# In-degrees of graphs 33 to 128 from a second load of the adjacency and GpSimd sums; Fourier coefficients stored in groups of four

## The chip, the cores and the metric

The kernel runs on one core of one Trainium2 chip. The metric is the device time of one execution in microseconds (us), lower being better. Times of before come from three runs; the profile is of one further execution. Engines are named as the profile names them: PE (TensorE matmuls), PEld (TensorE weight loads), DVE (VectorE), ACT (ScalarE), POOL (GpSimd), SP (SyncE, which issues most DMAs).

## The reference

128 graphs of 128 nodes with 256 features (x), and a weighted adjacency adj of 128 x 128 per graph, pass through two layers, each followed by a residual and a layer norm. All arithmetic is float32. Cut to what matters here:

```python
# layer 0, on x (128 graphs, 128 nodes, 256) and adj (128, 128, 128)
in_degrees = sum(adj, axis=-1)                       # one number per graph and node
norm  = (in_degrees + 1e-06) ** -0.5
f_hom = (adj @ ((x @ theta) * norm)) * norm
f_het = x @ W_h
gate  = sigmoid(x @ W_t + b_t)
x = layernorm(x + elu(gate * f_hom + (1 - gate) * f_het))

# layer 1
h      = relu(bn1(conv1(x)))                         # 1 x 1 convolution over the features
h      = bn2(conv2(h))                               # 17 taps along the nodes, 256 -> 256 features
x_conv = relu(h + x)
s      = x @ w_se.T + b_se
A      = exp(-pairwise_squared_distance(s)) * adj
x_nmp  = A @ relu(x @ w_msg.T + b_msg)
x = layernorm(x + GRU([x_conv, x_nmp], x))
```

## The kernel before

The kernel receives adj as `adjT` with its axes ordered (source node, graph, target node), so that a slice of it has source nodes on partitions. It works in three stages, and passes data between them through DRAM.

**Stage A** (`a_round`, lines 597 to 679, called for t = -1 to 63 at lines 681 to 683) takes the graphs in 64 pairs. Round t multiplies pair t by the three weights of layer 0 (`l0_project`), mixes it over the adjacency (`l0_mix`), and does later steps for earlier pairs: the gate, elu and norm of pair t-1, the store of x1 (the output of layer 0) of pair t-2, its reload in blocks (`load_back`, tile x1b) and its 32 x 32 block transposition on DVE (`l1_turn`, line 441, tile x1T), the first convolution of pair t-3 (`l1_front`), and, for pair t-4, the first half of the long convolution as a discrete Fourier transform over the nodes (`l1_analyse`, lines 481 to 492). That last step multiplies by a table of 136 frequencies and ACT copies the 2 x 136 coefficients of each graph from PSUM to the tile H (line 490). H stays in SBUF up to stage B. In most rounds four matmuls w_ps (`w_unit`, every second round) or a matmul wl_ps also transform conv2's weights.

The degrees of a pair are made one round ahead, in `l0_degrees` (lines 347 to 356): two TensorE transposes of its adjT tiles into a PSUM bank adj_ps (line 351), a DVE sum along the free axis (line 353), then an add and a power of -0.5 on POOL (lines 206 and 207). The result `norm` scales ACT's copy `hom` of the next round (line 380) and DVE's step behind the mix (line 402).

**Stage B** (lines 818 to 850) multiplies the coefficients by the transformed weights, one pair of frequencies k at a time, 68 in all. The stationary operand of a product is the 128 x 128 slice of H for one frequency m and one half c of the features, given by `coefs` (line 733). Each k has four such products (line 826), and all but k = 0 also two products whose stationary operand `hs` is a DVE sum of two slices of H (line 836).

**Stage C** (lines 1219 to 1258) does the way back of the transform, the message passing and the GRU. It does not touch H.

The order of the work in stage A is written out by hand for all five engines (`manual_schedule`, line 681), that of stage B for ACT and POOL, that of stage C for PE and DVE. Each engine runs its instructions in that order, and SP issues its DMAs in that order too. A float32 product issues two instructions on TensorE, each with its own weight load; a transpose issues one. H is made at t = 3 (line 670) in the space of the tiles of the setup:

```python
H = hpool.tile([P, NC, M, NB], F32, tag="H", name="H")   # 128 x (2 halves, 136 frequencies, 128 graphs)
```

Of the kernel before, what the change touches and what calls it, by code (L numbers as in the profile page):

```python
# [9 lines left out]
F32 = mybir.dt.float32  # L10
I32 = mybir.dt.int32
AF = mybir.ActivationFunctionType
ALU = mybir.AluOpType

P = 128
D = 256
NC = D // P
J = 2
# [8 lines left out]
M = L  # L27
# [3 lines left out]
DEG_EPS = 1e-6  # L31
# [3 lines left out]
def gnn_layers_kernel(ctx: ExitStack, tc: tile.TileContext, a: dict, out: bass.AP):  # L35
# [10 lines left out]
    nc = tc.nc  # L46
    x, adjT = a["x"], a["adjT"]
    NB = x.shape[0]
# [21 lines left out]
    ident = const.tile([P, P], F32, tag="ident", name="ident")  # L70
# [21 lines left out]
    K, Q = 32, P // 32  # L92
# [22 lines left out]
    for name, width, parts, pattern, base, mult in (  # L115
# [5 lines left out]
        i = setup.tile([P, width], I32, tag=f"{name}_i", name=f"{name}_i")  # L121
# [5 lines left out]
    def bank(name):  # L127
        return ps.tile([P, 512], F32, tag="ps", name=name)

    st = {}  # L130
# [225 lines left out]
        inv_sqrt(norm, norm, DEG_EPS, J)  # L356


    def l0_project(p, between, beside):
        s = st[p]  # L360
        xT, norm = s["xT"], s["norm"]
        hom = wf.tile([P, J, D], F32, tag="hom", bufs=2, name=f"hom_{p}")
        het = wk.tile([P, J, D], F32, tag="het", bufs=2, name=f"het_{p}")
        gate = wk.tile([P, J, D], F32, tag="gate", bufs=2, name=f"gate_{p}")
        pg = bank(f"gate_ps_{p}")
        for j in range(J):
            if j == 1:
                between()
            pf = bank(f"f_ps_{p}_{j}")
            for c in range(NC):  # L370
                nc.tensor.matmul(  # L371
                    pf, lhsT=xT[:, c, nodes(j)], rhs=w0[:, c, 0 : 2 * D],
                    start=(c == 0), stop=(c == NC - 1),
                )
            for c in range(NC):
                nc.tensor.matmul(  # L376
                    pg[:, j * D : (j + 1) * D], lhsT=xT[:, c, nodes(j)],
                    rhs=w0[:, c, 2 * D : 3 * D], start=(c == 0), stop=(c == NC - 1),
                )
            nc.scalar.activation(hom[:, j, :], pf[:, 0:D], AF.Copy, scale=norm[:, j : j + 1])  # L380
            nc.scalar.activation(het[:, j, :], pf[:, D : 2 * D], AF.Copy)
        beside()
        nc.vector.tensor_tensor(
            gate, pg.rearrange("p (j e) -> p j e", j=J),
            b_t.unsqueeze(1).to_broadcast([P, J, D]), ALU.add,
        )

        nc.scalar.activation(gate, gate, AF.Tanh, scale=0.5)
        s.update(hom=hom, het=het, gate=gate)
# [91 lines left out]
    def l1_analyse(p):  # L481
        h = st[p]["h"]
        for j in range(J):
            pa = bank(f"coef_ps_{p}_{j}")
            for c in range(NC):
                nc.tensor.matmul(  # L486
                    pa[:, c * M : (c + 1) * M], lhsT=h[:, j, c * P : (c + 1) * P], rhs=A,
                    start=True, stop=True,
                )
            nc.scalar.activation(  # L490
                H[:, :, :, p * J + j], pa[:, 0 : NC * M].rearrange("p (c m) -> p c m", c=NC), AF.Copy
            )


# [95 lines left out]
    H = None  # L590
    E = mybir.EngineType

    SOON = 3
    norms, ways = batch_norms(), way_back()
    tables = table(AT2, (node, lag))

    def a_round(t):
        nonlocal H
        def on(q, work):
            if 0 <= q < NP:  # L600
                work(q)

        def between():
            on(t - 1, l0_gate)
            on(t - 3, l1_turn)
            on(t - 4, l1_analyse)

        def beside():
            if 0 <= t <= SOON:
                l0_turn(t + 1)  # L610
            on(t - 1, l0_elu)
            if 0 <= t < SOON:
                l0_degrees(t + 1)

        if t > 1 and t % 2 == 1 and t + 1 < NP:
            load_blocks(t + 1, 2)
        l0_project(t, between, beside) if t >= 0 else between()
        on(t - 1, l0_norm)
        if t == 0:
            load_blocks(2, 2)  # L620
        if t == -1:
            next(tables)
        if not 0 <= t <= SOON:
            on(t + 1, l0_turn)
        on(t - 3, l1_front)
        on(t - 2, x1_store)
        if t > 0:
            load_x(t)
        if t + 2 < NP:
            if 2 <= t + 2:  # L630
                load(t + 2)
            if 3 <= t < 3 + FS:
                leftover_table(t - 3)
            if t == FS:
                v_load(0)
        else:
            on(t - 2, load_back)
            m_load(t + 2 - NP)
        if t - 1 in units:
            w_store(units[t - 1])  # L640
        if t - 1 in units_v:
            v_store(units_v[t - 1])
            if units_v[t - 1] + 1 < NV:
                v_load(units_v[t - 1] + 1)
        if t + 2 < NP:
            on(t - 2, load_back)
        on(t - 3, x1T_store)
        if not 0 <= t < SOON:
            on(t + 1, l0_degrees)
        if t == -1:  # L650
            next(tables, None)
        if t == 0:
            nc.sync.dma_start(conv1_w[:, :, 0:D], a["conv1_wT"].rearrange("(p c) e -> p c e", c=NC))
            nc.sync.dma_start(conv1_w[:, :, D:], a["w_seT"].rearrange("(p c) e -> p c e", c=NC))
            next(norms)
        if t == 1:
            next(norms)
            next(ways)
        if t == NP // 2:
            nc.scalar.dma_start(w_msg, a["w_msgT"].rearrange("(p c) e -> p c e", c=NC))  # L660
            nc.scalar.dma_start(b_msg, a["L1_gnn_b_msg"].partition_broadcast(P))
        on(t, l0_mix)
        if t == 2:
            next(norms, None)
        if t in (4, 5):
            next(ways, None)
        if t == SOON:
            sctx.close()
            hpool = hstack.enter_context(tc.tile_pool(name="hpool", bufs=1))
            H = hpool.tile([P, NC, M, NB], F32, tag="H", name="H")  # L670
        if 0 <= t < 2:
            w_load(t)
        if t - 1 in units and units[t - 1] + NW < NU:
            w_load(units[t - 1] + NW)
        if t in units_v:
            v_unit(units_v[t])
        if t in units:
            if t + 1 < NP:
                w_unit(units[t])
# [51 lines left out]
    pb = cpool("psB", 6, bctx, space=PSUM)  # L731

    def coefs(m, c):
        return H[:, c, m, :]

    left = cw.tile([P, NB, KD], F32, tag="left", name="left")
    right = cw.tile([P, NB, KD], F32, tag="right", name="right")
# [80 lines left out]
    with tc.manual_schedule(engines={E.Activation, E.Pool}):  # L818
        for k in range(M // 2):
            w = wb.tile([P, 2, NC, D], F32, tag="w", name=f"wb_{k}")  # L820
            nc.sync.dma_start(w, w_d[k].rearrange("s p c o -> p s c o"))
            py = pb.tile([P, 2, D], F32, tag="py", name=f"y_ps_{k}")
            y = yb.tile([P, 2, D], F32, tag="y", name=f"yb_{k}")
            for blk in range(2):
                for c in range(NC):
                    nc.tensor.matmul(  # L826
                        py[:, blk, :], lhsT=coefs(blk if k == 0 else 2 * k + 1 - blk, c),
                        rhs=w[:, blk, c, :], start=(c == 0), stop=(c == NC - 1),
                    )
            if k == 0:  # L830
                nc.vector.tensor_copy(y, py)
            else:
                ws = yb.tile([P, NC, D], F32, tag="ws", bufs=2, name=f"ws_{k}")
                nc.gpsimd.tensor_tensor(ws, w[:, 0], w[:, 1], ALU.add)  # L834
                hs = yb.tile([P, NC, NB], F32, tag="hs", bufs=2, name=f"hs_{k}")
                nc.vector.tensor_tensor(hs, H[:, :, 2 * k, :], H[:, :, 2 * k + 1, :], ALU.add)
                pz = pb.tile([P, 2, D], F32, tag="py", name=f"z_ps_{k}")
                for c in range(NC):
                    nc.tensor.matmul(  # L839
                        pz[:, 0, :], lhsT=hs[:, c, :], rhs=ws[:, c, :],  # L840
                        start=(c == 0), stop=(c == NC - 1),
                    )
                z = yb.tile([P, D], F32, tag="z", bufs=2, name=f"zb_{k}")
                nc.scalar.activation(z, pz[:, 0, :], AF.Copy, scale=-0.5)
                nc.vector.tensor_tensor(y, py, z.unsqueeze(1).to_broadcast([P, 2, D]), ALU.add)
            nc.sync.dma_start(y_d[:, 2 * k : 2 * k + 2, :], y)
            if k > 3 and k % 3 == 0:
                next(rest, None)
        for _ in rest:
            pass  # L850
# [369 lines left out]
    with tc.manual_schedule(engines={E.PE, E.DVE}):  # L1220
# [10 lines left out]
        half = l1_synth(0)  # L1231
        for g in range(NG):
# [8 lines left out]
            sums = l1_project(g + 1) if 2 <= g + 1 < NG else None  # L1241
# [59 lines left out]
```

## Time and profile before

| what | value |
|---|---|
| median of 3 runs | 1948.97 us (1948.71 to 1949.96) |
| profiled execution: time / span | 1949.05 us / 1947.3 us |
| granted TensorE clock, mean | 0.998 |
| PE busy | 1932.2 us, 99% of the span |
| PEld busy | 1324.2 us, 68% |
| DVE busy | 1497.8 us, 77% |
| ACT busy | 744.5 us, 38% |
| POOL busy | 674.3 us, 35% |
| bytes read from / written to HBM | 173.00 MB / 104.86 MB |

The profile gives the busy time of each engine, the chain of work that ended last, groups of instructions by line, and the instructions in order of time. An instruction of PE or PEld is one instruction of the hardware; since matmuls overlap, the duration of one is longer than the step from its start to the start of the next. The chain of work in order of time shows the steps, and a time on PE is worked out from these. Stage A lies at 0 to 645 us, stage B at 645 to 825 us, stage C from there to the end.

### The profile page before, as it was taken

The numbers are of one execution on the slowest core, as the hardware profiler recorded it, in microseconds if no ns is written. First come the engines' busy times: TensorE is split into PE (matmuls) and PEld (weight loads), VectorE is DVE, ScalarE is ACT, GpSimd is POOL, SyncE is SP. The second block draws the span as 40 slices with busy tenths as digits, with TensorE's granted clock in tenths as the row PEclk, the third lists the DMA queues.
The fourth block names the chain that finished last, engine by engine and source line by source line (L and its number), as shares of the span: only waits on it lengthen the run. The fifth ranks groups of instructions, "written<-read, shape, count | busy, mean of one in ns | idle before, by whom it ended". The sixth has DMA issues, their size and how long they took to land.

```text
span 1947.3 us, 26718 instructions
## 1 busy us (share of the span) xinstructions
PE 1932.2 (99%) x8533; PEld 1324.2 (68%) x8533; DVE 1497.8 (77%) x3024; ACT 744.5 (38%) x1497; POOL 674.3 (35%) x891
## 2 busy tenths in 40 slices
PE   9999999999999999999999999999999999999997
PEld 6666666666666888866666666666666666666664
DVE  8888888888888644477777777877777777777777
ACT  4666666666666311122322322222332232223222
POOL 2111111111111455544434434434443443443431
PEclk9999999999999999999999999999999999999999
DMA  6888777878776899952212221221221222121100
GB/s 175 229 231 234 225 230 221 240 225 231 222 226 202 292 341 331 314 174 83 83 53 74 72 72 60 78 66 56 82 83 49 75 75 72 60 77 39 44 28 22
DMA packets 333572, 279.64 MB, mean 144 GB/s; under 512 B 149647, under 2 KB 275833, under 8 KB 333433
## 3 DMA queue, kind: packets, MB, share of 16 engines
q1 hardware_dynamic: 326729, 272.42, 45.7%
q10 hardware_dynamic: 6704, 5.52, 0.9%
q8 instruction: 69, 1.13, 0.2%
q14 instruction: 70, 0.57, 0.1%
HBM read 173.00 MB, written 104.86 MB: 143 GB/s over the span
## 4 chain that ended last, share of the span: by engine, by line
PE 93%; DVE 3%; DMA 1%; ACT 1%; POOL 1%; issue 1%; SPq 0%; POOLq 0%; ACTq 0%; DVEq 0%
PE g_ps L1150 43%; PE f_ps L371 10%; PE y_ps L826 6%; PE conv_ps L465 5%; PE gate_ps L376 5%; PE msg_ps L1006 4%; PE conv_ps L945 3%; PE z_ps L839 3%; PE nmp_ps L1084 3%; PE coef_ps L486 3%; PE mix_ps L397 2%; PE w_ps L502 2%; PE conv_ps L952 1%; PE wl_ps L529 1%; PE adj_ps L351 1%; PE dist_ps L1064 1%
## 5 line engine op out<-in xcount | busy, mean ns | idle before, releaser
L329 ACT ACTIVATE y<-y,nb_b,rstd_b 128x256 f32<-128x256 f32 x128 | 70.0, 593 | 561.6 <-DVE nb_b L327 561.6
L371 PE MATMUL f_ps<-w,xT 128*128 128x512 f32 x512 | 243.9, 599 | 1.8 <-DMA w<-in_L_gnn_W_h 1.0
L1211 POOL TENSOR_TENSOR u<-u,p 128x512 f32<-128x512 f32 x63 | 80.0, 1270 | 244.2 <-DVE p L1191 244.2
L371 PEld LDWEIGHTS f_ps<-w,xT 128*128 128x128 f32 x512 | 89.9, 189 | 99.3 <-issue 66.3
L1150 PE MATMUL g_ps<-t_h,sh 128*128 128x384 f32 x384 | 156.8, 490 | 0.0
L1150 PE MATMUL g_ps<-t_c,sc 128*128 128x384 f32 x384 | 155.2, 486 | 0.0
L1150 PE MATMUL g_ps<-t_m,sm 128*128 128x384 f32 x384 | 155.2, 486 | 0.0
L206 POOL TENSOR_SCALAR rstd_a<-mv_a 128x2 f32<-128x2 f32 x64 | 12.4, 193 | 379.9 <-DVE mv_a L320 379.9
L376 PEld LDWEIGHTS gate_ps<-w,xT 128*128 128x128 f32 x512 | 97.3, 190 | 67.8 <-issue 54.1
L376 PE MATMUL gate_ps<-w,xT 128*128 128x256 f32 x512 | 131.4, 379 | 0.0
L826 PE MATMUL y_ps<-wb,H 128*128 128x256 f32 x544 | 128.3, 379 | 0.0
L834 POOL TENSOR_TENSOR ws<-wb 128x512 f32<-128x512 f32 x67 | 94.9, 1418 | 85.0 <-PE z_ps L839 54.0
L465 PE MATMUL conv_ps<-conv_w,x1T 128*128 128x259 f32 x512 | 122.6, 381 | 0.0
L826 PEld LDWEIGHTS y_ps<-wb,H 128*128 128x128 f32 x544 | 103.4, 190 | 14.0
L380 ACT ACTIVATE hom<-f_ps,norm 128x256 f32<-128x256 f32 x128 | 60.8, 475 | 125.2 <-PE f_ps L371 123.9
L1111 ACT ACTIVATE o<-o 128x1024 f32<-128x1024 f32 (+1 forms) x65 | 67.6, 1040 | 107.0 <-POOL o L1212 58.8
L1150 PEld LDWEIGHTS g_ps<-t_c,sc 128*128 128x128 f32 x384 | 73.0, 190 | 50.9
L1150 PEld LDWEIGHTS g_ps<-t_m,sm 128*128 128x128 f32 x384 | 73.0, 190 | 50.9 <-DVE sm L1100 0.2
L465 PEld LDWEIGHTS conv_ps<-conv_w,x1T 128*128 128x128 f32 x512 | 96.9, 190 | 14.6
L1150 PEld LDWEIGHTS g_ps<-t_h,sh 128*128 128x128 f32 x384 | 71.7, 190 | 48.7
L1150 PE MATMUL g_ps<-w_hhT_w,cx1T 128*128 128x384 f32 x256 | 104.6, 492 | 0.0
L1150 PE MATMUL g_ps<-w_ihT_w,xcT 128*128 128x384 f32 x256 | 103.0, 486 | 0.0
(247 smaller groups left out, 4430.4 us busy)
## 6 DMA issues: line engine op xcount, KB each, us to landing
wb<-w_d SPq DMA_DIRECT2D x68, 512.0 KB
w_d<-w_o SPq DMA_DIRECT2D x32, 1024.0 KB
y_d<-yb SPq DMA_DIRECT2D x68, 256.0 KB
x<-in_x SPq DMA_DIRECT2D x64, 256.0 KB
x_d<-x SPq DMA_DIRECT2D x64, 256.0 KB
cx1T<-x1T_d SPq DMA_DIRECT2D x64, 256.0 KB
yt<-y_d SPq DMA_DIRECT2D x32, 512.0 KB
cx<-x_d SPq DMA_DIRECT2D x32, 512.0 KB
```

The costliest lines, as they stand in the source:

```text
L329: nc.scalar.activation(dst[:, q, :], src[:, q, :], AF.Identity, bias=nb[:, q : q + 1], scale=rstd[:, q : q + 1],)
L371: nc.tensor.matmul(pf, lhsT=xT[:, c, nodes(j)], rhs=w0[:, c, 0 : 2 * D], start=(c == 0), stop=(c == NC - 1),)
L376: nc.tensor.matmul(pg[:, j * D : (j + 1) * D], lhsT=xT[:, c, nodes(j)], rhs=w0[:, c, 2 * D : 3 * D], start=(c == 0), stop=(c == NC - 1),)
L380: nc.scalar.activation(hom[:, j, :], pf[:, 0:D], AF.Copy, scale=norm[:, j : j + 1])
L465: nc.tensor.matmul(ph[:, 0 : D + CO], lhsT=s["x1T"][:, c, nodes(j)], rhs=conv1_w[:, c, :], start=(c == 0), stop=(c == NC - 1),)
L486: nc.tensor.matmul(pa[:, c * M : (c + 1) * M], lhsT=h[:, j, c * P : (c + 1) * P], rhs=A, start=True, stop=True,)
L826: nc.tensor.matmul(py[:, blk, :], lhsT=coefs(blk if k == 0 else 2 * k + 1 - blk, c), rhs=w[:, blk, c, :], start=(c == 0), stop=(c == NC - 1),)
L834: nc.gpsimd.tensor_tensor(ws, w[:, 0], w[:, 1], ALU.add)
L1006: nc.tensor.matmul(pm[:, pr * P : (pr + 1) * P], lhsT=s["fh"][i][:, pr, :], rhs=factors["g"][i], start=True, stop=True, skip_group_check=True,
L1111: nc.scalar.activation(rz, rz, AF.Tanh, scale=0.5)
L1150: nc.tensor.matmul(pg[:, lo : lo + 3 * P], lhsT=s[f"f{kind}"][i][:, pr, :], rhs=factors[kind][i], start=(k == 0), stop=(k == 2), skip_grou ...
L1211: nc.gpsimd.tensor_tensor(u4, u2, p5, add)
```

## The change

For pairs 0 to 15 the degrees are made as before. For pairs 16 to 63 they come in three waves w = 1, 2, 3 of 32 graphs (K = 32, Q = 4):

- `degrees_load`: eight DMAs per wave, issued on SP, load adjT a second time, with the 32 graphs of the wave on partitions. Each of four groups of 32 partitions holds another quarter of the source nodes. A DMA is 256 KB: 32 partitions, 16 source nodes each, 512 bytes per node. Wave 1 is loaded in rounds 4 to 11, one DMA per round, waves 2 and 3 in the even rounds 12 to 42.
- The loads go to a part of H that is not written until the last 32 graphs come (`spare`).
- `degrees_add`: POOL adds the 32 rows of a wave up to one, in seven adds of 128 x 512 and one each of 128 x 256 and 128 x 128, at most two steps of them per round.
- `degrees_make`, in rounds 15, 30 and 46: one product on TensorE with a 0/1 matrix `pick` adds the four quarters and turns the result to nodes on partitions (128 x 32), DVE adds the epsilon, and POOL takes the power of 32 columns at once. Slices of this are the `norm` of 16 pairs.

So that the spare part has rows of 512 contiguous bytes, H gets another layout: instead of the 128 graphs of one frequency side by side, groups of four frequencies stand together for each graph. A slice of H that stage B uses as stationary operand, or that DVE adds, now has a step of 16 bytes from graph to graph, where it was contiguous. ACT's copy into H writes runs of four values, where it wrote single values 512 bytes apart.

```diff
+    def spare(at, n):
+        return H[:, at : at + n, NB - K :, :].rearrange("p r b i -> p r (b i)")
+
+    def degrees_begin():
+        n = 2 * K
+        sums["pick"], sums["root"] = (spare(n + i, 1)[:, 0, 0:K] for i in range(2))
+        nc.gpsimd.memset(sums["root"], -0.5)
+        nc.gpsimd.tensor_tensor(sums["pick"], ident[:, 0:K], ident[:, K : 2 * K], ALU.add)
+        for q in range(2, Q):
+            nc.gpsimd.tensor_tensor(sums["pick"], sums["pick"], ident[:, q * K : (q + 1) * K], ALU.add)
+
+    def degrees_rows(w):
+        return spare((w - 1) % 2 * K, K)
+
+    def degrees_norm(w):
+        return H[:, NC * M // HI - 1, NB - K :, w]
+
+    def degrees_load(w, i):
+        q, n = i % Q, K // 2
+        at = slice(i // Q * n, i // Q * n + n)
+        v = adjT.rearrange("(q s) b n -> q b s n", q=Q)
+        nc.sync.dma_start(
+            degrees_rows(w)[q * K : (q + 1) * K, at, :], v[q, w * K : (w + 1) * K, at, :]
+        )
+
+    def degrees_add(w, i):
+        rows_ = degrees_rows(w)
+        def add(at, n):
+            nc.gpsimd.tensor_tensor(rows_[:, 0:n], rows_[:, 0:n], rows_[:, at : at + n], ALU.add)
+        if i % Q == Q - 1:
+            half = K // 2
+            for at in range(i // Q * half, (i // Q + 1) * half, HI):
+                if at:
+                    yield add(at, HI)
+        if i == 2 * Q - 1:
+            add(2, 2)
+            yield add(1, 1)
+
+    def degrees_make(w):
+        t = bank(f"deg_ps_{w}")
+        nc.tensor.matmul(
+            t[:, 0:K], lhsT=degrees_rows(w)[:, 0, :], rhs=sums["pick"], start=True, stop=True
+        )
+        norm = degrees_norm(w)
+        nc.vector.tensor_scalar(norm, t[:, 0:K], DEG_EPS, None, ALU.add)
+        nc.gpsimd.tensor_tensor(norm, norm, sums["root"], ALU.pow)
+        for p in range(w * K // J, (w + 1) * K // J):
+            st[p]["norm"] = norm[:, p * J % K : p * J % K + J]
...
@@ l1_analyse
-                H[:, :, :, p * J + j], pa[:, 0 : NC * M].rearrange("p (c m) -> p c m", c=NC), AF.Copy
+                H[:, :, p * J + j, :],
+                pa[:, 0 : NC * M].rearrange("p (r i) -> p r i", i=HI), AF.Copy,
...
+    parts = {4 + i: (1, i) for i in range(2 * Q)}
+    parts.update({12 + 2 * i: (2 + i // (2 * Q), i % (2 * Q)) for i in range(4 * Q)})
+    made = {max(t for t in parts if parts[t][0] == w) + 4: w for w in range(1, NB // K)}
...
@@ a_round
         on(t - 3, x1T_store)
-        if not 0 <= t < SOON:
+        if t in parts:
+            degrees_load(*parts[t])
+        if not 0 <= t < SOON and t + 1 < K // J:
             on(t + 1, l0_degrees)
+        if t in made:
+            degrees_make(made[t])
...
         on(t, l0_mix)
+        if t - 1 in parts:
+            adds.append(degrees_add(*parts[t - 1]))
+        for _ in range(2):
+            while adds and next(adds[0], adds) is adds:
+                adds.pop(0)
...
-            H = hpool.tile([P, NC, M, NB], F32, tag="H", name="H")
+            H = hpool.tile([P, NC * M // HI, NB, HI], F32, tag="H", name="H")
+            degrees_begin()
...
     def coefs(m, c):
-        return H[:, c, m, :]
+        return H[:, (c * M + m) // HI, :, m % HI]
...
-                nc.vector.tensor_tensor(hs, H[:, :, 2 * k, :], H[:, :, 2 * k + 1, :], ALU.add)
+                rows_k = slice(2 * k // HI, NC * M // HI, M // HI)
+                ha, hb = (H[:, rows_k, :, (2 * k + i) % HI] for i in range(2))
+                nc.vector.tensor_tensor(hs, ha, hb, ALU.add)
```

## The prediction

> **What bounds the kernel now.** I read the page's busy times and chain first, then the stages as time windows, then the chain in order of time inside stages A and B.
>
> ```profile
> PE 1932.2 (99%) x8533; PEld 1324.2 (68%) x8533; DVE 1497.8 (77%) x3024; ACT 744.5 (38%) x1497; POOL 674.3 (35%) x891
> ...
> PE 93%; DVE 3%; DMA 1%; ACT 1%; POOL 1%; issue 1%; SPq 0%; POOLq 0%; ACTq 0%; DVEq 0%
> ```
>
> TensorE is busy throughout, and the chain runs on it. The windows of stages A (without its start), B and C (columns: window, its length, busy us of each engine with counts, clock, DMA share, GB/s):
>
> ```profile
> 50.00:645.00 595.00, 594.34 (x2592) 403.30 (x2591) 505.35 (x1101) 390.04 (x906) 105.04 (x236) 1.00 0.79 227
> 645.00:825.00 180.00, 179.88 (x837) 157.63 (x836) 85.94 (x154) 30.62 (x79) 98.03 (x72) 1.00 0.94 322
> 825.00:1947.00 1122.00, 1110.90 (x4925) 732.78 (x4924) 862.52 (x1663) 298.68 (x456) 456.31 (x539) 1.00 0.22 69
> ```
>
> In A and B no engine but PE is full: DVE has 15% free in A and 52% in B, POOL 82% in A. So a step taken off PE is a gain until another engine or a load becomes late, and a step that becomes longer on PE is a loss in full. The chain in order of time gives the steps (start, us, what); first a round of stage A, then stage B, then the only matmuls of this program whose stationary operand isn't contiguous:
>
> ```profile
> 311.32 1.75 PE conv_ps L465 x8
> 313.07 0.22 PE adj_ps L351 x2
> 313.29 0.86 PE mix_ps L397 x4
> ```
>
> ```profile
> 702.05 1.73 PE y_ps L826 x8
> 703.77 0.86 PE z_ps L839 x4
> ```
>
> ```profile
> 634.27 0.47 PE x1T_ps L451 x4
> ```
>
> Two degree transposes take 0.22 us of an unbroken chain, 0.108 us each. A product of stage B (256 columns) steps by 1.73/8 = 0.216 us; its weight load runs beside the product before it, so up to 0.216 us it costs nothing. The transposes at L451 read every second float and step by 0.118 us instead of 0.108.
>
> **The change, part by part.** The sum is made against the profiled execution: 1949.05 us, of which 1947.3 are span; the median of the runs, 1948.97, is 0.08 less, so the same sum serves for it.
>
> Removed from PE: 48 pairs x 2 transposes = 96 x 0.108 = 10.4 us. All of it lies in the unbroken chain: -10.4. Also removed are 48 DVE sums of 0.41 us (line 353) and 48 x (0.19 + 0.70) = 43 us of POOL; neither bounds, so 0. Without adj_ps a round takes one PSUM bank less from the ring of 8, so each bank is reused later in the work than before: no new wait.
>
> Added to PE: three products, two instructions each. The nearest row is a 128-column product of stage C, 0.11 us per instruction: 6 x 0.11 = +0.7.
>
> Added to POOL: 21 adds of 128 x 512. The row below gives 1.27 us (1.42 for the same shape at line 834): 27 to 30 us, and some 4 us for the six short ones. At most two fall in a round, queued behind the power for `norm` and ahead of `rstd_a`. POOL waits there 379.9/64 = 5.9 us per round, so 2 x 1.42 = 2.8 us fit: 0. If they did not, DVE would wait at `nb_a`, and with it everything behind it on DVE. The power of 32 columns: by the rows, 0.70 us for two columns and 1.02 for four, 0.16 us a column, so 0.70 + 30 x 0.16 = 5.5 us, three times. It lies in the same gap. In rounds 30 and 46 its result is needed one or two rounds later. In round 15 the next round's first `hom` needs it, and in the trace that one starts only 1.7 to 2.2 us after the power of 0.70 ends; so ACT is late once by 5.5 - 0.7 - 1.9 = 2.9 us. ACT is 66% busy, and the mix that needs the second `hom` starts some 2 us after that one is made: of 2.9 us I leave 1.0 on PE (ends 0 and 2.9).
>
> ```profile
> L1211 POOL TENSOR_TENSOR u<-u,p 128x512 f32<-128x512 f32 x63 | 80.0, 1270 | 244.2 <-DVE p L1191 244.2
> ```
>
> ```profile
> L207 POOL TENSOR_TENSOR norm<-norm,neg_half x64: 697/697/772, 7.2 to 620.9; 128x2 f32<-128x2 f32 x64
> ...
> L207 POOL TENSOR_TENSOR scale<-scale,neg_half x1: 1019/1019/1019, 14.8 to 14.8; 128x4 f32<-128x4 f32 x1
> ```
>
> Added to SP and the DMA engines: 24 loads of 512 packets. The queue row gives 0.457 x 16 x 1947.3 us / 326729 = 44 ns a packet, so a load takes 512 x 44 ns / 16 = 1.4 us of all engines. In rounds 4 to 11 the DMA share rises from 0.79 to about 0.94, later by 0.07. On SP a load of as many packets (xb) takes 0.49 us in the median, up to 1.86. It stands behind the round's x1b and x1T loads and stores and ahead of the next round's xb, x1 store and x1b, so it can delay x1b, on which DVE's transposition waits:
>
> ```profile
> q1 hardware_dynamic: 326729, 272.42, 45.7%
> ```
>
> ```profile
> L441 DVE STREAM_TRANSPOSE x1T<-x1b x62: 702/704/727, 32.6 to 631.1; 128x512 f32<-128x512 f32 x62
> its engine sat idle before it (us, times) until:
>   DMA x1b<-x_d: 3.0, 3
> ```
>
> Today DVE waits there only 3.0 us in all, but the margin is thin: taken from the landings in the trace, x1b lies ready 0.1 to 6 us ahead, and less than 1.4 us in about a quarter of the rounds. Behind it there are 2.2 to 3.7 us from the end of the transposition to the convolution on PE in nearly all rounds. So a load that is 1.4 us late is mostly absorbed: I take +1.0 for all 24 (ends 0, and 10 for the rival below). adjT itself, which the mix now waits for directly, lies ready some 10 us ahead: 0.
>
> ACT's copy into H (line 490): 666 ns for 272 values. Contiguous copies take 384 ns for 256 (line 844) and 599 for 512 (line 505), so 0.84 ns a value and 397 for 272; with runs of four I expect 400 to 666 ns. ACT doesn't bound: 0. DVE's `hs` (426 ns) reads with a step of 16 bytes: the nearest row, line 759, adds 128 values with steps of 12 and 32 bytes in 384 ns, some 0.75 ns a value over contiguous, so at worst 67 x 0.19 = 13 us on a DVE that has 94 us free in stage B and makes `hs` ahead: 0.
>
> The weight loads of H are the open price. 544 loads in stage B read with a step of 16 bytes. No row shows that step on PE. The nearest are these:
>
> ```profile
> L351 PEld LDWEIGHTS adj_ps<-ident,adjT x128: 137/139/152, 5.3 to 619.4; 128*128 128x128 f32 x128
> ...
> L451 PEld LDWEIGHTS x1T_ps<-ident,x x8: 194/201/209, 633.9 to 640.9; 128*128 128x128 f32 x8
> ...
> L826 PEld LDWEIGHTS y_ps<-wb,H x544: 190/190/190, 648.1 to 823.1; 128*128 128x128 f32 x182
> ...
> L490 ACT ACTIVATE H<-coef_ps x128: 621/666/761, 42.4 to 646.8; 128x272 f32<-128x272 f32 x128
> ```
>
> With a step of 8 bytes a load takes 201 instead of 139 ns, and the matmuls behind step by 0.118 us: 128 values are read in about 118 ns. Low end: a step of 16 bytes costs what 8 do, 118 < 216 ns, 0 (a gain is excluded, as PE already steps by its products). Middle: twice that, 236 ns, 544 x 0.020 = +10.9 us; ACT's single values at L490, which take (666 - 397)/272 = 0.99 ns more each, 2.2 times as much, point this way, but on another engine and with 512 bytes between. High end: four times a contiguous read, 4 x 0.108 = 432 ns, 544 x 0.216 = +118 us. I take 0, because L451 is the same engine and operand.
>
> The Trainium skill, in "SBUF — State Buffer", section "Door 1: The DMA port swizzle", speaks against this: SBUF is read in lines of 16 bytes, and an access needs at least two hits in a line to run at full rate. A step of 16 bytes has one. The same note calls a step of four float32 values free. As an estimate from the page, its first rule makes the load twice as slow as L451's, and the sum would be 10.9 us more; its second makes the sum as it stands. L451, with two hits in a line, is already slower than contiguous, which the page does not say.
>
> Sum: -10.4 + 0.7 + 1.0 + 1.0 + 0 = -7.7, so 1949.05 - 7.7 = 1941.3 us (-0.4%). A difference under 0.2%, 3.9 us, can't be told from none.
>
> **Rivals.** (1) Half rate: the weight loads of H take 224 to 236 ns, 4.4 to 10.9 us more, 1945.7 to 1952.2. For it: L490, and that L451 already loses. It eats the whole gain at 216 + 7.7/0.544 = 230 ns. (2) The other side: the weight loads become the bound of stage B, at 250 ns and more. For it: L451 shows that a step costs TensorE's weight load more (139 to 201 ns) than a moving operand, whose step of 8 bytes (line 529) makes 0.45 us out of 0.43; the stage has the DMA at 0.94 beside it. Against it: nothing in the trace reads slower than 2.2 times. At 300 ns it is 544 x 0.084 = 46 us, 1987; at 432 ns 2059. (3) The loads make x1b late: ten of the 24 cost 1 us on PE, 1950 us. For it: margins under 0.5 us in several rounds; against it: the 2.2 to 3.7 us behind them. (4) That nothing is taken off PE is excluded: the built program has 93 products and transposes less on PE and the same order otherwise on all engines.
>
> **How the numbers follow.** Forecast 0.43, 1939.4 (only the products added) to 1944; rival 1 0.23, of which 0.04 faster, 0.13 same, 0.06 slower; rival 2 0.22, from 1960 on; rival 3 0.12, a third each way. Faster 0.43 + 0.04 + 0.04 = 0.51, same 0.17, slower 0.06 + 0.22 + 0.04 = 0.32. The range from 1937.5 (ACT's shorter copies take away 2 us of small waits) to 1966 holds the forecast, rivals 1 and 3 and the start of rival 2, about 0.81. The forecast's own range is 1937.5 to 1945.
>
> **What would show it.** Stage A shorter by 8 to 10 us, with x1b waits on DVE still a few us; line 351 with 32 instructions; the power of 32 columns at 5 to 6 us; the product of stage B still stepping by 0.216 us. Wrong if it steps by more, which stage B's window shows directly: 1.2 us for each 2 ns, or if DVE's waits for x1b grow to tens of us.

## The result, and the profile after

The changed kernel takes 1957.41 us in the median (1955.80 to 1959.49, six runs) against 1948.89 us of the kernel before (1948.47 to 1949.96, six runs): a ratio of 1.0044, with a 95% interval of 1.0031 to 1.0057. The change costs 8.5 us where a gain of 7.7 was forecast. The profiled execution of after took 1959.49 us, 1957.7 of them span, 10.4 us more span than the one of before.

The busy times and the chain, from the page of after:

```profile
PE 1934.3 (99%) x8443; PEld 1340.2 (68%) x8443; DVE 1504.4 (77%) x2979; ACT 720.7 (37%) x1497; POOL 694.3 (35%) x829
...
PE 88%; DVE 6%; DMA 2%; ACT 2%; POOL 1%; issue 1%; SPq 0%; POOLq 0%; DVEq 0%; ACTq 0%
```

PE has 90 instructions fewer and is still busy 2.1 us longer, so some of those that are left have become longer. And the chain has left PE: its share falls from 93 to 88%, that of DVE rises from 3 to 6. So there are two things to look for. The windows of stages A, B and C, with the columns used before (engine busy times, clock, DMA share, GB/s):

```profile
50.00:645.00 595.00, 587.11 (x2505) 395.48 (x2502) 503.51 (x1061) 368.81 (x910) 113.29 (x172) 1.00 0.84 238
645.00:825.00 180.00, 180.00 (x796) 172.52 (x795) 92.82 (x149) 29.41 (x76) 103.78 (x67) 1.00 0.90 303
825.00:1947.00 1122.00, 1121.39 (x4973) 742.75 (x4971) 861.57 (x1655) 297.90 (x456) 460.07 (x540) 1.00 0.23 72
```

In the window of A PE now stands still for 595 - 587.1 = 7.9 us, where it was 0.7. In the window of B, which is a little shorter than the stage now, PE is full, PEld has gone from 157.6 to 172.5 us, and 796 instructions are done in the time of 837. The starts of the stages divide the 10.4 us: the first product y_ps starts at 649.78 us instead of 648.36 (+1.4, where -7.7 was forecast); from there to the end of the last z_ps it takes 185.24 us instead of 176.18 (+9.1); stage C takes 1122.7 us in both.

Stage B first. The chain in order of time, in after (start, us, what):

```profile
700.89 1.86 PE y_ps L897 x8
702.76 0.86 PE z_ps L912 x4
```

Eight products y_ps take 1.86 us instead of 1.73, 0.233 instead of 0.216 us each; z_ps, whose stationary operand stays contiguous, takes 0.86 as before. There are 68 such eights: 68 x 0.13 = 8.8 of the 9.1 us. The weight loads of that line:

```profile
L897 PEld LDWEIGHTS y_ps<-wb,H x544: 308/329/329, 649.6 to 833.5; 128*128 128x128 f32 x182
```

329 ns in the record instead of 190. A record is longer than the room that a load takes: the transposes that read every second float show 201 ns and step by 118, 83 ns less. By that difference a record of 329 ns would make a step of 246 ns; measured are 233. So the weight load may now be the bound of the stage; the first three experiments test it.

Stage A. Two stretches of the chain of after, the first behind a load of x1b, the second behind DVE:

```profile
60.91 0.04 issue
60.95 4.71 DMA x1b<-x_d
65.66 0.03 issue
...
133.55 1.65 DVE het L469
135.23 1.39 DVE gate L470
136.64 0.64 ACT gate L471
```

The reload of x1b ends the wait of DVE at 65.7 us, and once more at 85.9 (a piece of 3.38 us); the longest such piece in the chain of before is 3.92 us. At 133.55 `het` and `gate` on DVE take 1.65 and 1.39 us; in the kernel before every one of them took 0.69 and 0.43. The groups of these lines and of the adds (duration min/median/max in ns, first and last start in us), the first two for 50 to 645 us:

```profile
L469 DVE SCALAR_TENSOR_TENSOR het<-hom,het x60: 691/692/1646, 52.2 to 633.9; 128x512 f32<-128x512 f32 x60
...
L327 DVE SCALAR_TENSOR_TENSOR nb_a<-mv_a,rstd_a x60: 160/161/1237, 57.9 to 640.6; 128x2 f32<-128x2 f32 x60
...
L393 POOL TENSOR_TENSOR H<-H x27: 462/1282/1997, 93.2 to 457.4; 128x512 f32<-128x512 f32 x21, 128x256 f32<-128x256 f32 x3, 128x128 f32<-128x128 f32 x3
...
L411 POOL TENSOR_TENSOR H<-H x3: 5468/5472/5477, 163.8 to 467.9; 128x32 f32<-128x32 f32 x3
```

The medians of `het` and `nb_a` are as before, their maxima are not: 1646 instead of 693 ns, and 1237 instead of 163 for an operation on two values per partition. In the whole of stage A 19 operations of DVE are longer than usual, by 16.7 us in sum, and each of them overlaps one of POOL's adds (L393); in the trace of before there is none. In wave 1 the adds stand behind POOL's power for `norm` and meet `het` (5 times) and `gate` (4 times); from round 16 on that step is gone from POOL, the adds run right behind `rstd_a` and meet `nb_a` (10 times). Where DVE's operation came first, it is the add that is long: 1.6 to 2.0 us.

Not every operation beside an add is longer. Two adds in after with what DVE does meanwhile, and then the same operations in before, where POOL has no add:

```profile
201.62 2.64 POOL L393 TENSOR_TENSOR H<-H 128x512 f32<-128x512 f32 x2
201.69 1.23 DVE L327 SCALAR_TENSOR_TENSOR nb_a<-mv_a,rstd_a 128x2 f32<-128x2 f32 x1
202.84 0.71 DVE L498 STREAM_TRANSPOSE xT<-xb 128x512 f32<-128x512 f32 x1
203.46 0.73 DVE L526 TENSOR_TENSOR h<-conv_ps,shift 128x256 f32<-128x256 f32 x2
204.10 0.86 DVE L459 SCALAR_TENSOR_TENSOR hom<-mix_ps,H,het 128x256 f32<-128x256 f32 x2
```

```profile
302.00 0.16 DVE L327 SCALAR_TENSOR_TENSOR nb_a<-mv_a,rstd_a 128x2 f32<-128x2 f32 x1 [0.18 <-POOL rstd_a L207]
302.08 0.70 DVE L441 STREAM_TRANSPOSE xT<-xb 128x512 f32<-128x512 f32 x1
302.70 0.71 DVE L469 TENSOR_TENSOR h<-conv_ps,shift 128x256 f32<-128x256 f32 x2
303.96 0.88 DVE L402 SCALAR_TENSOR_TENSOR hom<-mix_ps,norm,het 128x256 f32<-128x256 f32 x2 [0.21 <-PE mix_ps L397]
```

`xT`, a transposition, and `h` and `hom`, with an input in PSUM, keep their length beside an add; so they do in the whole of stage A (8, 12 and 6 times).

The waits that have grown (engine, line, releaser: us in all, times, longest):

```profile
DVE x1T L498 <- DMA x1b<-x_d: 8.4, 4, 3.1
...
ACT hom L437 <- POOL H L411: 5.0, 1, 5.0
...
PE f_ps L428 <- DVE xT L498: 4.3, 4, 1.5
```

Against the median step of its products, PE loses in the rounds at 65 to 91 us (x1b) 3.0 us, at 100 to 113 and at 152 us (adds) 2.5, at 173 to 184 us (the power that `hom` waits for) 1.9, and at 349 to 371 us 1.5 (mostly one round in which x1b is 1.3 us late and `nb_a` then takes 1.24); of these 9 us, 0.7 were there before.

Another 2.5 us go in the first 12 us of the execution. PE stands still there for 2.37 us until a load lands (1.05 in the profile of before), and the four products behind take 3.52 us instead of 1.95; the granted clock from 6 to 12 us is 0.72, in the profile of before 1.00. The profiles of three of the experiments (the whole change with groups of two, the adds behind the power of `rstd`, the product one round later) start in the same way, with a clock of 0.87 over the first 13 us; those of the others, with the same work there, show 1.00. So the start isn't counted for the change, and it fits that the profiled execution lies 2.1 us above the median.

### The profile page after: what moved, and what is told of

Its sections match the earlier page's. It is cut to its first block, busy times and chain, and to the rows that moved or that the text cites. A ratio compares the mean times of both kernels' runs of the same rounds, so it can differ in the third digit from the quotient of the medians.

```text
span 1957.7 us, 26392 instructions
## 1 busy us (share of the span) xinstructions
PE 1934.3 (99%) x8443; PEld 1340.2 (68%) x8443; DVE 1504.4 (77%) x2979; ACT 720.7 (37%) x1497; POOL 694.3 (35%) x829
## 4 chain that ended last, share of the span: by engine, by line
PE 88%; DVE 6%; DMA 2%; ACT 2%; POOL 1%; issue 1%; SPq 0%; POOLq 0%; DVEq 0%; ACTq 0%
PE g_ps L1223 43%; PE f_ps L428 8%; PE y_ps L897 6%; PE msg_ps L1079 4%; PE conv_ps L522 4%; PE gate_ps L433 4%; PE z_ps L912 3%; PE conv_ps L1018 3%; PE nmp_ps L1157 3%; PE coef_ps L543 2%; PE mix_ps L454 2%; PE w_ps L560 1%; PE conv_ps L1025 1%; DMA x1b<-x_d 1%; PE wl_ps L587 1%
## 5 line engine op out<-in xcount | busy, mean ns | idle before, releaser
L897 PE MATMUL y_ps<-wb,H 128*128 128x256 f32 x544 | 137.7, 397 | 0.0
L905 POOL TENSOR_TENSOR ws<-wb 128x512 f32<-128x512 f32 x67 | 105.8, 1581 | 83.5 <-PE z_ps L912 58.2
L897 PEld LDWEIGHTS y_ps<-wb,H 128*128 128x128 f32 x544 | 131.9, 326 | 1.7
L909 DVE TENSOR_TENSOR hs<-H 128x256 f32<-128x256 f32 x67 | 49.0, 732 | 81.8 <-PE z_ps L912 81.0
```

The lines of the kernel that those rows point to most:

```text
L897: nc.tensor.matmul(py[:, blk, :], lhsT=coefs(blk if k == 0 else 2 * k + 1 - blk, c), rhs=w[:, blk, c, :], start=(c == 0), stop=(c == NC - 1),)
```

## The experiments

Theory: two separate causes, the weight loads of H in stage B, and in stage A loads and adds that make other work late. Rivals were that the weight loads are not slow by their step but by the traffic beside them, and that in stage A one cause alone explains the loss. All medians are compared with the kernel before on the same chip, 1948.8 to 1949.1 us there. The times of the stages are those of the profiled executions: A up to the first y_ps (648.4 us before), B from there to the end of the last z_ps (176.2 before). The three kernels that leave loads or adds out compute wrong degrees for graphs 33 to 128; they only show times.

**Groups of four alone.** The kernel before with the new layout of H, and nothing of the degrees.

```diff
-            H = hpool.tile([P, NC, M, NB], F32, tag="H", name="H")
+            H = hpool.tile([P, NC * M // HI, NB, HI], F32, tag="H", name="H")
-        return H[:, c, m, :]
+        return H[:, (c * M + m) // HI, :, m % HI]
```

> Only the layout of H is changed (groups of four), the degrees stay as before. Theory L (the weight loads with a step of 16 bytes are longer than the products that hide them): the product of stage B steps by 0.233 us as in the changed kernel, stage B lasts 185 instead of 176 us, the time is 1958 us. Rival (stage B is longer because hs on DVE, 732 instead of 426 ns, holds up the z products, or because of what the new degrees leave behind): the step stays 0.216 or only z waits, and without the degrees the time is 1949 to 1952 us. Stage A is the same to 1 us in both.

Measured: 1957.25 us (1956.98 to 1957.55), ratio 1.0040 [1.0028, 1.0052]. Stage A 647.3 us, 1.0 shorter, stage B 185.75, 9.6 longer. The weight loads of y_ps:

```profile
L828 PEld LDWEIGHTS y_ps<-wb,H x544: 308/329/330, 647.1 to 831.6; 128*128 128x128 f32 x182
```

The layout alone gives the whole loss of stage B, and its 8.2 us are nearly the whole loss of the change. So the work on the degrees, all of it, nets to about nothing.

**Groups of two.** The same with one number changed, a step of 8 bytes.

```diff
-    HI = 4
+    HI = 2
```

> The same with groups of two, so that the weight loads have a step of 8 bytes, two values in a 16-byte line. Theory L with a price per line of 16 bytes: the load's record is 200 to 255 ns, the step stays 0.216 us, 1949 us (within 2). Rival, a price per value for any step: the record stays near 326 ns and the time near 1958 us.

Measured: 1948.98 us (1948.26 to 1951.08), ratio 0.9999 [0.9991, 1.0008]. The weight loads, and the chain in stage B:

```profile
L828 PEld LDWEIGHTS y_ps<-wb,H x544: 194/196/198, 647.3 to 822.7; 128*128 128x128 f32 x182
```

```profile
701.20 1.73 PE y_ps L828 x8
702.92 0.86 PE z_ps L843 x4
```

196 ns and a step of 0.216 us: the loads hide again, with the same traffic beside them. The step of the operand is the cause.

**Groups of eight**, a step of 32 bytes.

```diff
-    HI = 4
+    HI = 8
```

> Only the layout of H is changed, in groups of eight: the weight loads have a step of 32 bytes, the degrees stay as before. Price per 16-byte line touched: one line per value as with a step of 16, so the record stays near 329 ns, the step of the product near 0.233 us, 1957 us. Rival, a price that grows with the distance: a record of 450 ns or more, a step of 0.35 us or more, 2020 us or more.

Measured: 1960.88 us (1960.19 to 1961.36), ratio 1.0059 [1.0047, 1.0072]; stage B 188.5 us.

```profile
L828 PEld LDWEIGHTS y_ps<-wb,H x544: 312/337/339, 647.0 to 834.2; 128*128 128x128 f32 x182
```

Contiguous 190 ns (with the product as the bound), 8 bytes 196, 16 bytes 329, 32 bytes 337: the price comes between 8 and 16 bytes and hardly grows beyond. Twice as many values apart does not cost twice as much. Eight products take 1.92 us in the chain, 0.240 each: from 16 to 32 bytes the record grows by 8 ns and the step by 7, so the products follow the weight loads.

**Without the adds.** The changed kernel, but the loaded rows are not summed.

```diff
         if t - 1 in parts:
-            adds.append(degrees_add(*parts[t - 1]))
+            pass
```

> The changed kernel without POOL's 27 adds: the products take one of the 32 rows, so the degrees of graphs 33 to 128 are wrong. Loads, powers, layout stay. Theory P (the adds take the SBUF access that DVE's operations with two SBUF inputs need): DVE's long het and gate operations (1.66 and 1.39 us) are back at 0.69 and 0.44, and the loss of rounds 8, 12 to 14 goes: about 4 us less than the changed kernel, 1953.5 us. Rival D (the loads make x1b late and the adds are hidden): unchanged, 1957 us.

Measured: 1953.84 us (1951.45 to 1954.59), ratio 1.0021 [1.0012, 1.0030]; stage A 641.5 us, stage B 185.3. No operation of DVE is longer than usual. The wait for x1b is there:

```profile
DVE x1T L498 <- DMA x1b<-x_d: 11.5, 9, 2.9
```

**Without the loads.** POOL fills the rows instead and still adds them.

```diff
-        nc.sync.dma_start(
-            degrees_rows(w)[q * K : (q + 1) * K, at, :], v[q, w * K : (w + 1) * K, at, :]
-        )
+        if w < 3 and i % Q == Q - 1:
+            for r in range(at.start, at.stop, HI):
+                nc.gpsimd.memset(degrees_rows(w)[:, r : r + HI, :], 0.5)
```

> The changed kernel without the 24 loads: POOL fills the rows with a constant by sixteen memsets of 128 x 512 in rounds 7, 11, 18 and 26, so the degrees of graphs 33 to 128 are wrong; adds, powers, layout stay. Theory D: the waits for x1b in rounds 6 and 8 go and with them about 3 us, 1954.5 us. If the adds and the power alone make the loss of stage A (theory P): 1957 us.

Measured: 1955.10 us (1952.44 to 1955.98), ratio 1.0026 [1.0015, 1.0036]; stage A 642.2 us, stage B 185.5. DVE's operations are longer by 16.8 us in sum, as in the changed kernel, and PE waits behind them; the wait for x1b is nearly gone:

```profile
DVE x1T L498 <- DMA x1b<-x_d: 1.7, 2, 1.2
...
PE f_ps L428 <- DVE xT L498: 3.3, 4, 1.5
```

**Without both.** POOL fills one row of a wave, and nothing is loaded or added.

```diff
-        nc.sync.dma_start(
-            degrees_rows(w)[q * K : (q + 1) * K, at, :], v[q, w * K : (w + 1) * K, at, :]
-        )
+        if w < 3 and i == 0:
+            nc.gpsimd.memset(degrees_rows(w)[:, 0, :], 0.5)
...
-            adds.append(degrees_add(*parts[t - 1]))
+            pass
```

> The changed kernel with neither loads nor adds (one row per wave is filled with a constant, so the degrees of graphs 33 to 128 are wrong); products, powers of 32 columns and the layout in groups of four stay. If loads and adds make the loss of stage A together (each alone gave back 2.3 and 3.5 us of some 10): stage A is 8 us or more shorter than before apart from the power of round 15 (about 1.5 us), and with the 8.2 us of the layout the time is 1949 to 1950.5 us. Rival, the transposes were not worth 10.4 us in the first place: 1953 us or more, without stalls of PE in stage A.

Measured: 1948.74 us (1947.66 to 1952.36), ratio 1.0000 [0.9991, 1.0009]; stage A 639.1 us, stage B 185.3. The group of `het` and two waits:

```profile
L468 DVE SCALAR_TENSOR_TENSOR het<-hom,het x60: 691/692/693, 50.2 to 623.2; 128x512 f32<-128x512 f32 x60
```

```profile
ACT hom L436 <- POOL H L410: 5.0, 1, 5.0
DVE x1T L497 <- DMA x1b<-x_d: 4.1, 3, 2.3
PE f_ps L427 <- DVE xT L497: 0.8, 2, 0.5
```

With loads and adds gone, taking the transposes off PE gains what it should: 1948.74 against 1957.25 of the layout alone, 8.5 us. On that footing the loads alone cost 1953.84 - 1948.74 = 5.1 us, the adds alone 1955.10 - 1948.74 = 6.4, and both 1957.41 - 1948.74 = 8.7. They are both causes. The sum of the two would be 11.5, but with intervals of about 2 us on each median it isn't shown that they overlap: by the ratios they cost 4.1 and 5.1 us, and the profiled executions say the opposite. There PE stands still between 50 us and stage B for 0.8 us without both, 2.8 with the loads alone, 4.2 with the adds alone and 7.9 with both, so 2.0 and 3.4 alone against 7.1 together. Which of the two is larger stays open too, and so does why x1b comes late beside the loads, by its place in SP's queue or by slower transfers.

**The whole change with groups of two.** The rows of 512 bytes become rows of 256, in twice as many packets, and the product is two products of 64 rows.

```diff
-    HI = 4
+    HI = 2
...
-        v = adjT.rearrange("(q s) b n -> q b s n", q=Q)
+        v = adjT.rearrange("(q s) b (h m) -> q h b s m", q=Q, h=2)
...
-        nc.tensor.matmul(
-            t[:, 0:K], lhsT=degrees_rows(w)[:, 0, :], rhs=sums["pick"], start=True, stop=True
-        )
+        for h in range(2):
+            nc.tensor.matmul(
+                t[64 * h : 64 * h + 64, 0:K], lhsT=degrees_rows(w)[:, h * K, :], rhs=sums["pick"],
+                start=True, stop=True,
+            )
```

> The whole change with groups of two: a row of 128 target nodes is kept as two halves of 64, the loads have packets of 256 bytes instead of 512 (1024 per load), adds and powers as in the change, two products of 64 rows per wave. The weight loads cost nothing, so 8.2 us less than the change: 1949.2 us. If the smaller packets make x1b later still: 1951 to 1955 us.

Measured: 1948.60 us (1945.17 to 1950.24), ratio 0.9997 [0.9988, 1.0005]; stage B 176.6 us, stage A 648.4. Stage B is mended. Stage A gives next to nothing: its profile has the late start described above, which makes it 1.5 us later at 20 us than with groups of two alone (647.5), and it has the same long operations on DVE (16.8 us in sum).

**Adds behind the power of `rstd`, and the long power in four pieces.** Made on the kernel with groups of two.

```diff
-        nc.gpsimd.tensor_tensor(norm, norm, sums["root"], ALU.pow)
+        for c in range(0, K, 8):
+            nc.gpsimd.tensor_tensor(norm[:, c : c + 8], norm[:, c : c + 8], sums["root"][:, c : c + 8], ALU.pow)
...
@@ a_round: this loop goes from behind l0_mix to the place ahead of l0_norm
+        for _ in range(2):
+            while adds and next(adds[0], adds) is adds:
+                adds.pop(0)
```

> Groups of two, and in each round POOL's adds are issued right behind rstd, where DVE for some 4 us mostly reads PSUM or one operand, instead of behind norm, where DVE's five operations with two SBUF inputs follow; the power is cut into four of 8 columns. Theory P: DVE's long operations go, the loss of rounds 8 to 14 and of round 15 with them, about 4 to 5 us less than the same with the old places, 1944.5 us. If adds behind rstd meet DVE's work as before: within 1 us of the version with groups of two alone.

Measured: 1948.02 us (1945.61 to 1949.69), ratio 0.9992 [0.9983, 1.0001]; stage A 647.1 us, again with the late start. That misses the 1944.5 us of the theory: DVE's long operations have not gone but moved, 15 of them, all at `nb_a`, 14.3 us in sum. The wait of `hom` for the long power is gone, and another takes its place, the degree product on the last add:

```profile
PEld deg_ps L408 <- POOL H L394: 4.2, 3, 1.5
PE deg_ps L408 <- POOL H L394: 3.0, 3, 1.1
```

PE stands still there for 1.1, 1.4 and 1.3 us.

**Without wave 1.** Groups of two, adds behind the power of `rstd`; graphs 33 to 64 keep their transposes, so 64 instead of 96 go.

```diff
-    parts = {4 + i: (1, i) for i in range(2 * Q)}
-    parts.update({12 + 2 * i: (2 + i // (2 * Q), i % (2 * Q)) for i in range(4 * Q)})
+    parts = {12 + 2 * i: (2 + i // (2 * Q), i % (2 * Q)) for i in range(4 * Q)}
...
-        if not 0 <= t < SOON and t + 1 < K // J:
+        if not 0 <= t < SOON and t + 1 < 2 * K // J:
```

> Groups of two, adds behind rstd, and no wave 1: pairs 0 to 31 keep their transposes, so 64 instead of 96 go (-6.9 us, +0.4 for the products), and no loads come in rounds 4 to 11, where x1b was late. Theory D (the early loads): 1943 to 1944 us, with no x1b wait above those of before. If late loads cost as much as the early ones: 1946 to 1949 us.

Measured: 1946.42 us (1944.89 to 1948.61), ratio 0.9987 [0.9978, 0.9996]; stage A 644.4 us, stage B 176.0. That is above the 1943 to 1944 us expected. With a third of the transposes back, it is 2.2 us faster than the whole change with groups of two and 1.6 faster than the version just before, on the same chip, but the intervals overlap. It fits that wave 1 cost more than its 32 transposes gave, as its loads came one per round instead of one in two; that is not shown by itself. DVE still waits 5.3 us for x1b (3.0 in the kernel before). Two waits of the degree product on the last add are left, 0.95 and 1.29 us of PE.

**The product one round later**, to get rid of these.

```diff
-    made = {max(t for t in parts if parts[t][0] == w) + 4: w for w in range(2, NB // K)}
+    made = {max(t for t in parts if parts[t][0] == w) + 5: w for w in range(2, NB // K)}
```

> As e8 (groups of two, adds behind rstd, no wave 1), but the product of a wave is issued one round later (31 and 47), since in e8 PE waited 1.0 and 1.3 us there for POOL's last adds, which had also moved by a round. If that wait is what is left: 1944 to 1945 us. If the adds cost the rest elsewhere: 1946 us.

Measured: 1949.04 us (1947.05 to 1951.79), ratio 1.0000 [0.9991, 1.0009]. The wait for the adds is gone, and the power of 32 columns has moved to where the next `hom` needs it:

```profile
ACT hom L440 <- POOL H L414: 7.3, 2, 4.9
```

PE loses 1.2, 1.6 and 1.1 us between 324 and 349 us. It was a miss: the wait was moved, not removed.

**The last add one round earlier**, the product where it was: a round's add is queued behind the same round's `rstd`.

```diff
@@ a_round: ahead of the loop that runs the adds, instead of behind l0_mix
+        if t - 1 in parts:
+            adds.append(degrees_add(*parts[t - 1]))
```

> Groups of two with no product in wave 1, as in the run with groups of two and only late products; the one difference: a round's add is put behind that same round's rstd instead of being held for the next round, so the last add stands one round earlier, and the product stays at rounds 30 and 46. Theory 'the wait of the degree product on the last add (0.95 and 1.29 us in the run before this one) is what is left to gain': about 2 us below that run's 1946.4 us, 1944.3 us, with neither wait above 0.3 us. Rival 'the work of GpSimd only moves, and what comes next in its queue is late instead' (as when the product was made one round later: 1949.0 us): 1946 to 1949 us, with new stalls of PE of about 1 us each beside the powers of 32 columns.

Measured: 1944.77 us (1943.48 to 1948.79), ratio 0.9981 [0.9972, 0.9990]; stage A 642.9 us, stage B 176.9. The weight load of the degree product waits for no add:

```profile
PEld deg_ps L408 <- issue: 0.5, 2, 0.3
...
DVE x1T L501 <- DMA x1b<-x_d: 3.5, 5, 1.4
```

DVE's operations are longer by 9.6 us in sum, all at `nb_a`, and PE shows nearly nothing of it: it stands still for 1.0 us between 50 us and stage B, in the kernel before for 0.7. The time is what the theory gave.

**The same with the long power in four pieces.**

```diff
-        nc.gpsimd.tensor_tensor(norm, norm, sums["root"], ALU.pow)
+        for c in range(0, K, 8):
+            nc.gpsimd.tensor_tensor(norm[:, c : c + 8], norm[:, c : c + 8], sums["root"][:, c : c + 8], ALU.pow)
```

> The same, with the power of 32 columns (5.47 us) in four powers of 8 columns each, by rounds. Theory 'the long power in one piece is late for ACT': if the run beside this one shows a wait of ACT on that power, this one is up to 1.5 us below it, 1943 to 1944.5 us; if it shows none, the two are equal within 1 us. Rival 'the adds beside DVE's operations with two inputs in SBUF are what costs': no difference between the two, and DVE's excess over the kernel before stays near 14 us of operations in both.

Measured: 1944.65 us (1943.13 to 1946.32), ratio 0.9977 [0.9968, 0.9986]. No difference from the one beside it, which had no wait on that power. DVE's excess is 9.6 and 9.5 us; the 14 us of the expectation belong to the versions with wave 1. These two kernels are faster than both kernels of this case, by 4.0 and 4.1 us against the one before.

## Why the prediction was wrong

The forecast was 1941.3 us and faster; the kernel is slower, at 1957.4. Term by term, from differences of medians:

| step | predicted | measured | from |
|---|---|---|---|
| transposes off, three products on, power late once | -10.4 + 0.7 + 1.0 = -8.7 | -8.5 | without both - layout alone |
| layout of H: weight loads, ACT's copies | 0 | +8.2 | layout alone - before |
| loads of adjT, x1b late | +1.0 | +5.1 alone, 2.3 beside the adds | without adds - without both; after - without loads |
| adds on POOL | 0 | +6.4 alone, 3.6 beside the loads | without loads - without both; after - without adds |

The first row, the layout and the two together (8.7) make 8.4, against the 8.5 measured; they have to, as each is taken from where the one before ends. The parts of the 8.7 are uncertain by some 2 us or more.

**The weight loads of H.** This is the largest failed step: "I take 0, because L451 is the same engine and operand." The same engine was right to look at, but L451 reads with a step of 8 bytes, and I let it stand for 16. The price was a middle case that the prediction had (236 ns, +10.9 us, rival 1); measured are 233 ns and +9.1 us in stage B. ACT's row L490 had pointed to about this price, on another engine and with another step. L451, whose step of 8 bytes takes 118 ns for what takes 108 contiguous, could not: one row at one step doesn't say where the price comes. The sign named for it, a longer step of the product, did show; "1.2 us for each 2 ns" should read 544 x 2 ns = 1.1 us. The Trainium skill, in "SBUF — State Buffer", section "Door 1: The DMA port swizzle", had the edge in the right place: lines of 16 bytes, and two hits in a line for the full rate. The runs agree for the weight load: 196 ns at two hits, 329 at one, 337 where every second line is left out (though at two hits L451 already steps by 118 ns instead of 108). The same note's other half, that four float32 values are a free step, was not true of this load.

**The adds.** "2 x 1.42 = 2.8 us fit: 0. If they did not, DVE would wait at `nb_a`". The adds did fit into POOL's queue; the error was to look for their price only there. An add and an operation of DVE ran one after the other although they had different engines: `het` 1.65 instead of 0.69 us, `gate` 1.38 instead of 0.43, `nb_a` 1.23 instead of 0.16. `nb_a` was the place named, but there it doesn't wait in a queue: it has been issued and takes the length of the add. The profile of before had a hint that went unread: `hs` in stage B took 1491 ns at most with a median of 426, where POOL's `ws` had started first. The Trainium skill, in "SBUF — State Buffer", section "Who interferes with whom", states the rule: an operation of DVE with two inputs in SBUF and one of GpSimd that reads SBUF contend for a shared pair of ports (as does a `tensor_scalar` in a 2-port mode), and the one that comes second waits until the other is done. The trace agrees, also in that the add is the longer one (1.6 to 2.0 us) where DVE was first, and in that the transposition and DVE's operations with an input in PSUM keep their length.

**The loads.** The mechanism was named (rival 3), the size was not: +1.0 taken, 5.1 measured alone. "Mostly absorbed" rested on "2.2 to 3.7 us" of room behind the transposition "in nearly all rounds", and it failed at 65 and 86 us, where x1b was 3.1 us late at most and PE stood still for 2.1 and 0.9 us. The exceptions lay just there: in the profile of before the room is 0.8 us at 62 us and 0.5 at 82, and wave 1's loads go into these rounds. The 3.0 us are what this profile shows; where the rest of the 5.1 falls is open.

**The power of 32 columns** takes 5.47 us, where 5.5 was worked out from two rows. Its delay is 5.0 us instead of 2.9, and PE pays 1.0 to 1.9 of it (0.55 + 0.42 without loads and adds, 1.5 + 0.4 with them).

**Right besides:** the gain on PE, and ACT's copies into H, 397 ns instead of 666. They were costed at nothing; the layout's stage A is 0.9 to 1.2 us shorter in all three group sizes, which fits them and is not tested by itself. `hs`, in the changed kernel, costs more than the bound (626 ns median instead of 426, mean 732) and stays hidden:

```profile
L909 DVE TENSOR_TENSOR hs<-H x67: 599/626/1700, 650.6 to 829.6; 128x256 f32<-128x256 f32 x67
```

**The chances.** 0.43 for the forecast and 0.45 for the two cases of slow weight loads, and each priced on the rest going as planned. That two of the small terms fail at once, 8.7 us in all beside the 8.2 of the layout, was in none of the cases.

## What to carry to other kernels

Before a stationary operand gets a stride, look for a weight load with that very stride, or measure one: here 8 bytes between float32 values were free under a product of 216 ns, and 16 were not. Work put on an idle GpSimd has to be laid beside what DVE does at that moment, and a DVE operation whose maximum is far above its median is the sign to look for. A stage in which one engine is full and the others have small margins gives a gain back quickly: of the versions tried here, the change paid (4 us) only once its early third, where loads and adds came closest together, was left out and each step of POOL had a round to spare.

## What was not expected of the hardware

- TensorE's weight load of 128 x 128 float32 by the step between the columns' values: records of 190 ns (contiguous, under a product), 196 (8 bytes), 329 (16 bytes), 337 (32 bytes). The products over it step by 0.216, 0.216, 0.233 and 0.240 us (chain: 1.92 us for eight at 32 bytes).
- A 128 x 512 add on GpSimd that starts just before `het`, `gate` or `nb_a` on DVE adds 0.95 to 1.07 us to it, however short that is: 0.69 to 1.65, 0.43 to 1.38, 0.16 to 1.23 us. The transposition, and operations with an input in PSUM, are not touched.
- GpSimd's power costs by the column: 0.70 us for 2, 1.64 for 8, 5.47 for 32.
